# Attention with routed experts on one core: earlier routed chunks, sums over two steps, and an end in halves

## The chip, the core and the metric

The kernel runs on one core of a Trainium2 chip, as one launch. The metric is the device time of that launch in microseconds (us). Its engines are TensorE (PE, with weight loads as PEld), VectorE (DVE), ScalarE (ACT), GpSimd (POOL) and SyncE (SP, which here only issues DMAs). [...]

## The reference

The input x has 8 sequences of 512 tokens of 128 numbers. The output is x plus an attention layer plus a layer of experts, both fed with the same layer norm of x:

```python
xn = _layernorm(x)
# attention: 16 heads of 8 numbers, causal
w = softmax(q @ k.T / sqrt(8), masked below the diagonal)
attn = (w @ v) @ Wp + bp
# experts: the best 2 of 8 for each token, and one shared by all
ffn(x, g, u, d) = silu(x @ g.T) * (x @ u.T) @ d.T      # 352 hidden
routed = sum over the 2 chosen e of topw[e] * ffn(xn, expert e)
out = x + attn + ffn(xn, shared) + routed
```

## The kernel before

Tokens lie on the 128 partitions. A sequence has four tiles of 128 tokens (NC = 4), so there are 32 tiles (NT); `x_sb` holds them all in SBUF and collects the output: each part of the result is added into it.

**Steps.** The main loop runs over 32 sets n of four heads (a sequence b has four sets) and over five score tiles in each (`TILES`: two "wide", two "mixed", one "half"). That makes 160 steps, step = 5n + i. In a step, `weigh` lets TensorE fill a two-bank PSUM tile with scores (`fill`; the pool has a single buffer), and ScalarE takes one Exp over 1024 columns to `pT` (line 443). The diagonal blocks must be masked: in the first 40 steps TensorE adds a mask by small matmuls (L326), from step 40 (`BUSY`) GpSimd sets masked places to zero after Exp by an affine select (L451). In steps with i = 2, 4 and 0 of the next set, `attend` multiplies finished `pT` tiles by the values into the PSUM tile `av` (L466). The scores' row maxima, needed before a set's Exp, are made ahead by `look` for the step 11 later: TensorE matmuls into two banks (L365), two reduces on VectorE (L394, L400), and a cast on ScalarE that lays the mask down (L353). `shift` sends the maxima by three small DMAs into extra rows of q. The last maxima are taken in step 148.

**Attention's end.** After two sets, `evacuate` copies `av` to `o_sb` (ScalarE, L491); `divide` transposes it on TensorE (L500), takes reciprocals of the sums and multiplies (VectorE, L502, L506) into `a_new`. After a sequence's four sets, `turn` transposes `a_new` (L514) and copies it to `attT` (ScalarE, L515), and `join` multiplies by `wp_sb` (L537) and adds the product to `x_sb` (L541).

**Experts.** The work is a stream of 52 pairs of 128-row blocks: 13 shared pairs, 36 routed, 3 shared (`experts`). A pair has three chunks: TensorE gate and up matmuls (`gu`, one PSUM buffer, L611), a tanh on ScalarE (L616) and two VectorE operations (L617, L618). During the next pair's first two chunks it gets its two down projections (L638). A routed block's result is copied by ScalarE (L644) and scattered to a DRAM buffer `results` by GpSimd's indirect DMA (L622); a shared one is added to `x_sb` (L648). Where chunks run is set by a table: `chunks[step]` spreads k chunks evenly over a range of steps. The first chunk of a step stands after `look`, a second one at the step's end. Before: 39 shared chunks in steps -2 to 41, 108 routed in 42 to 145, 9 shared in 146 to 157.

**Collecting.** When all routed pairs are stored, each further step from the third on collects one sequence: two DMAs of 256 KB on SP's queue (`collect`, L706), which depend on all returns. `add_up` runs two steps (`LAG`) after, half a sequence a step, with a scalar_tensor_tensor on VectorE for each tile and choice (x += result * weight, L719). `due(step, f)` puts f into a step's side work, which `side` takes after that step's chunk and before up to two waiting down projections. `store` writes a sequence by SP (L726).

**After the last step** come the last attend and `evacuate`, the last pair's two down projections, what is still due (the last sums, `divide`, `turn`, `join`), and the stores of sequences 6 and 7.

The order on PE, DVE, ACT and SP is that of the program text. No planner moves it.

Of the kernel before, what the change touches and what calls it, by code (L numbers as in the profile page):

```python
# [11 lines left out]
F32 = mybir.dt.float32  # L12
# [3 lines left out]
ALU = mybir.AluOpType  # L16
# [9 lines left out]
P = 128  # L26
B, S, E = 8, 512, 128
H, D = 16, 8
NC = S // P
NT = B * NC  # L30
NG = H // 4
HH = H // 2
# [5 lines left out]
EARLY = 13  # L38
NE = 8
FF = 352  # L40
NF = 3
FP = NF * P
TOPK = 2
NP = TOPK * NT * P
BLK = P
MB = 2
# [4 lines left out]
BUSY = 40  # L51
# [3 lines left out]
LAG = 2  # L55
# [10 lines left out]
def attn_moe_kernel(  # L66
# [15 lines left out]
    nc = tc.nc  # L82
# [8 lines left out]
    x_sb = const.tile([P, NT, E], F32, name="x_sb")  # L91
# [8 lines left out]
    wp_sb = const.tile([E, E], F32, name="wp_sb")  # L100
# [22 lines left out]
    ident = const.tile([P, P], F32, name="ident")  # L123
# [4 lines left out]
    for i in range(NV):  # L128
        t = const.tile([P, NC, H, 32], F32, name=f"v_ext{i}")
# [6 lines left out]
    for i in range(NU):  # L136
        q = const.tile([P, HH, S], BF16, name=f"qs{i}")
        k = const.tile([P, HH, S], BF16, name=f"ks{i}")
# [19 lines left out]
    for m, sign in ((mask_q, 1), (mask_k, -1)):  # L158
        nc.gpsimd.memset(m, 0.0)
        nc.gpsimd.affine_select(  # L160
            out=m, in_=m, pattern=[[-sign, P]], compare_op=ALU.is_ge, fill=MASKED,
# [9 lines left out]
        out=before, in_=ones16, pattern=[[1, P]], compare_op=ALU.is_gt, fill=0.0,  # L171
# [6 lines left out]
    for e in range(NE):  # L178
# [5 lines left out]
        out=upto, in_=upto, pattern=[[1, NE], [-1, NE]], compare_op=ALU.is_ge, fill=0.0,  # L184
# [12 lines left out]
    attT = rows  # L197
    weight = const.tile([P, TOPK, NT], F32, name="weight")
# [8 lines left out]
    def pool(name, bufs, **kw):  # L207
        return ctx.enter_context(tc.tile_pool(name=name, bufs=bufs, **kw))
# [3 lines left out]
    at = pool("at", 2)  # L212
# [11 lines left out]
    def misc(shape, name, dtype=F32):  # L224
        return mi_ps.tile(shape, dtype, tag="mi", name=name)


    a_sb, in_dram, parts_of, first_dram = {}, {}, {}, []
# [64 lines left out]
    def fetch(u, h0=0, h1=HH):  # L293

        b, half = divmod(u, 2)
        heads = slice(half * HH + h0, half * HH + h1)
        rows_q, rows_k = in_dram[b]
        for r in range(3):
            nc.sync.dma_start(qs[u % NU][24 * r : 24 * r + 24, h0:h1], rows_q[:, heads])
        for r in range(3):  # L300
            d = nc.sync.dma_start(
                ks[u % NU][24 * r : 24 * r + 24, h0:h1], rows_k[8 * r : 8 * r + 24, heads]
            )
        return d.ins
# [134 lines left out]
    def weigh(n, kind, j, on_pool):  # L439

        ps = fill(n, kind, j, on_pool)
        pT = pr.tile([P, 2, S], F32, name="pT")
        last_exp[:] = [nc.scalar.activation(pT, ps, AF.Exp, scale=D**-0.5).ins]  # L443
        if on_pool:
            if kind == "half":
                diagonals = [pT.rearrange("p t (u k) -> p (t u) k", u=2)[:, :, :P]]
            else:
                diagonals = [pT[:, :, :P]] + ([pT[:, :, 3 * P :]] if kind == "mixed" else [])
            with tc.issue_after(sent[-1]):
                for d in diagonals:  # L450
                    nc.gpsimd.affine_select(  # L451
                        out=d, in_=d, pattern=[[0, d.shape[1]], [1, P]], compare_op=ALU.is_ge,
                        fill=0.0, base=0, channel_multiplier=-1,
                    )
        return pT
# [70 lines left out]
    def offset(b):  # L526
        xb = x_sb[:, ts(b, NC), :]
        with tc.issue_after(sent[-1]) if sent else ExitStack():
            nc.gpsimd.tensor_tensor(
                xb, xb, bias_sb.unsqueeze(1).to_broadcast([P, NC, E]), ALU.add  # L530
            )

    def join(b):

        ps = misc([P, NC, E], "p_ps")
        for c in range(NC):
            nc.tensor.matmul(  # L537
                ps[:, c], lhsT=attT[:, b * NC + c], rhs=wp_sb, start=True, stop=True
            )
        xb = x_sb[:, ts(b, NC), :]  # L540
        nc.vector.tensor_tensor(xb, ps, xb, ALU.add)  # L541


    stream = [("shared", j) for j in range(EARLY)]
# [155 lines left out]
    got = {}  # L700

    def collect(b):

        r = later_pools["got"].tile([P, TOPK, NC, E], F32, name="r")
        for i in range(TOPK):
            d = nc.sync.dma_start(  # L706
                r[:, i].rearrange("p c e -> p (c e)"),
                results[ds(i * NT * P + b * S, S)].rearrange("(p c) e -> p (c e)", p=P),
            )
            for x_ in returned:  # L710
                tc.add_manual_dep(d.ins, x_.name, SYNC, reason="any pair may be in any block")
        got[b] = r

    def add_up(b, c0, c1):

        for c in range(c0, c1):
            t = b * NC + c
            for i in range(TOPK):
                nc.vector.scalar_tensor_tensor(  # L719
                    x_sb[:, t, :], got[b][:, i, c], weight[:, i, t : t + 1], x_sb[:, t, :],  # L720
                    ALU.mult, ALU.add,
                )

    def store(b):

        nc.sync.dma_start(out[b].rearrange("(c p) e -> p c e", p=P), x_sb[:, ts(b, NC), :])  # L726
# [5 lines left out]
    total_steps = B * NG * NTILES  # L732
    ready = {}

    def due(step, f):
        ready.setdefault(step, []).append(f)
# [3 lines left out]
    def look(step, between=lambda: None):  # L740

        t = len(looked)
        if t >= total_steps:
            return lambda: None
        looked.append(step)
        n, i = divmod(t, NTILES)
        maxima(n, i, between)
        if i < NTILES - 1:
            return lambda: None
        if n == 0:  # L750
            return partial(shift_parts, n)
        if n < 4:
            return lambda: due(step + 1, partial(shift, n, shift_parts(n)))
        return lambda: first.setdefault(step + 2, []).append(partial(shift, n, shift_parts(n)))
# [16 lines left out]
    def begin(step):  # L771
        for f in first.pop(step, []):
            more = f()
            if more is not None:
                more()
# [310 lines left out]

    to_collect = list(range(B))

    first_step, routed_from, routed_to = -2, 42, 146
    chunks = {}  # L1090
    for a, z, k in (
        (first_step, routed_from, NF * EARLY),
        (routed_from, routed_to, NF * (NB // MB)),
        (routed_to, total_steps - 2, NF * (NT // MB - EARLY)),
    ):
        for m in range(z - a):
            chunks[a + m] = (m + 1) * k // (z - a) - m * k // (z - a)
# [6 lines left out]
    all_back = []  # L1104
# [6 lines left out]
    for t in range(FIRST):  # L1111
        step = t - FIRST
# [40 lines left out]
    for n in range(B * NG):  # L1153
        b, g = divmod(n, NG)
        waiting = []
        for i, (kind, j) in enumerate(TILES):
            step = n * NTILES + i
            begin(step)
            if step in fetches:
                fetch(fetches[step])  # L1160
            on_pool = step >= BUSY
            waiting.append((kind, j, weigh(n, kind, j, on_pool)))
            parts_then = look(step)
            some_chunks(step, False)
            if step in light:
                warm(5)
            parts_then()
            if step not in MORE and len(looked) < total_steps:
                prepare(*divmod(len(looked), NTILES))
            some_routing()  # L1170
            send_some()
            for f in late:
                f()
            late = []
            if i == 1 and n % 2 == 0:
                av = av_ps.tile([P, S], F32, name="av")
            if i in (1, 3, 4):
                late = [partial(attend, n, waiting, av)]
                waiting = []
            side(step, 2)  # L1180
            some_chunks(step, True)
            if step in MORE:
                look(step)()
                prepare(*divmod(len(looked), NTILES))
            if len(stored) == NB // MB:
                if not all_back:
                    for_routed.close()
                    later_pools["got"] = pool("got", 6)
                all_back.append(step)
            if to_collect and len(all_back) > 2:  # L1190
                at_b = to_collect.pop(0)
                collect(at_b)
                due(step + LAG, partial(add_up, at_b, 0, NC // 2))
                due(step + LAG + 1, partial(add_up, at_b, NC // 2, NC))

                if (at_b + 1) * NC <= MB * EARLY:
                    due(max(step + LAG + 2, last_shift), partial(store, at_b))
        if n % 2:
            late.append(partial(evacuate, n, av))
            due(step + 2, partial(divide, n))  # L1200
        if n % NG == 2 and b + 1 < B:
            due(step + 1, partial(offset, b + 1))
        if g == NG - 1:
            due(step + 3, partial(turn, b))
            due(step + 4, partial(join, b))
# [12 lines left out]
    for step in sorted(ready):  # L1218
        for f in ready[step]:
            more = f()  # L1220
            if more is not None:
                more()
    for b in to_collect:
        collect(b)
        add_up(b, 0, NC)
    for b in range(MB * EARLY // NC, B):
        store(b)


_OUT = (B, S, E)  # L1230
# [58 lines left out]
```

## Time and profile before

| | |
|---|---|
| runs | 620.67 us median of 3 (618.37 to 620.8) |
| profiled execution | 616.3 us, its span from first to last instruction 614.6 us |
| mean granted TensorE clock | 0.968 |
| busy: PE, DVE, ACT, POOL | 563.3, 463.3, 370.4, 244.0 us |
| Exp (L443), 160 of them | 164.1 us busy, 1026 ns each |
| sums of results (L719), 64 | 21.4 us busy |
| sums of products (L541), 8 | 5.4 us busy, 681 ns each |
| result loads (L706), 16 DMAs | 256 KB each |
| Exp of step 138 and of step 159 start | 533.6 and 596.6 us |

The profile gives one execution. A group's line has its source line, engine, operation and tiles, with count and durations in ns. In the digits over 40 slices each stands for 15.4 us, and 9 means 90% or more. In the timeline the first number is the start, the second the length, and the bracket tells how long the engine had been idle and what released it. Since each step has one Exp, in order, the rows of L443 date the steps.

### The profile page before, as it was taken

The numbers are of one execution on the slowest core, as the hardware profiler recorded it, in microseconds if no ns is written. First come the engines' busy times: TensorE is split into PE (matmuls) and PEld (weight loads), VectorE is DVE, ScalarE is ACT, GpSimd is POOL, SyncE is SP. The second block draws the span as 40 slices with busy tenths as digits, with TensorE's granted clock in tenths as the row PEclk, the third lists the DMA queues.
The fourth block names the chain that finished last, engine by engine and source line by source line (L and its number), as shares of the span: only waits on it lengthen the run. The fifth ranks groups of instructions, "written<-read, shape, count | busy, mean of one in ns | idle before, by whom it ended". The sixth has DMA issues, their size and how long they took to land.

```text
span 614.6 us, 13602 instructions
## 1 busy us (share of the span) xinstructions
PE 563.3 (92%) x4796; PEld 414.0 (67%) x4796; DVE 463.3 (75%) x1213; ACT 370.4 (60%) x668; POOL 244.0 (40%) x365
## 2 busy tenths in 40 slices
PE   6989598798999999999999999999999999999964
PEld 4656375566666677777776877777777877786533
DVE  7787867676768787777787778687788778876594
ACT  5735354463547666686667666586667766665530
POOL 9510444643557234333433344233434334433320
PEclk9989799998999999999999999999999999999986
DMA  7744244142143674838585785838585875720471
GB/s 219 229 117 172 95 109 109 37 131 78 37 121 110 197 225 135 233 106 251 178 240 159 223 233 166 217 93 250 178 218 194 238 232 145 215 96 3 138 223 51
DMA packets 52363, 98.38 MB, mean 160 GB/s; under 512 B 10054, under 2 KB 35530, under 8 KB 50136
## 3 DMA queue, kind: packets, MB, share of 16 engines
q1 hardware_dynamic: 46216, 83.78, 47.6%
q0 software_dynamic: 5360, 13.66, 6.4%
q8 instruction: 38, 0.62, 0.4%
q14 instruction: 29, 0.24, 0.1%
q10 hardware_dynamic: 720, 0.08, 0.1%
HBM read 73.36 MB, written 24.26 MB: 159 GB/s over the span
## 4 chain that ended last, share of the span: by engine, by line
PE 67%; ACT 6%; DVE 6%; issue 2%; POOL 0%; ACTq 0%; DVEq 0%
PE gu L611 19%; PE av L466 11%; PE y L638 11%; PE scT L322 9%; PE sc_diag L365 5%; PE sc_left L365 4%; DVE x_sb L719 3%; ACT pT L443 2%; PE qk_ps L239 2%; ACT sc_diag L353 2%; PE p_ps L537 1%; ACT th L616 1%; PE s_ps L585 1%; PE aT_ps L514 1%; PE mT_ps L423 1%
## 5 line engine op out<-in xcount | busy, mean ns | idle before, releaser
L443 ACT ACTIVATE pT<-scT 128x1024 f32<-128x1024 f32 x160 | 164.1, 1026 | 68.6 <-PE scT L322 27.3
L622 POOL DMA_INDIRECT results<-o,goes x72 | 73.1, 1015 | 129.7 <-ACT o L644 110.0
L451 POOL TENSOR_SCALAR_AFFINE_SELECT pT<-pT 128x256 f32<-128x256 f32 (+1 forms) x168 | 72.4, 447 | 118.7 <-ACT pT L443 115.6
L611 PE MATMUL gu<-sT,w 128*128 128x128 f32 x864 | 116.0, 277 | 2.3 <-PE sc_left L365 0.8
L394 DVE TENSOR_REDUCE peaks<-sc_diag 128x4 f32<-128x512 f32 x128 | 88.0, 688 | 38.1 <-PE sc_diag L365 25.7
L611 PEld LDWEIGHTS gu<-sT,w 128*128 128x128 f32 x864 | 108.0, 191 | 6.8 <-PE sc_diag L365 1.8
L322 PE MATMUL scT<-qs,ks 75*128 75x384 bf16 (+3 forms) x512 | 103.2, 303 | 3.9 <-ACT pT L443 3.8
L690 POOL DMA_INDIRECT slots<-rows_attT,slot x64 | 62.6, 979 | 81.2 <-issue 36.2
L616 ACT ACTIVATE th<-gu 128x256 f32<-128x256 f32 x156 | 59.8, 384 | 57.7 <-PE gu L611 39.7
L466 PE MATMUL av<-pT,v_ext 128*32 128x512 f32 (+3 forms) x1024 | 91.2, 452 | 1.0 <-POOL pT L451 1.0
L365 PEld LDWEIGHTS <-qs 72*128 72x128 bf16 x896 | 64.9, 98 | 38.8 <-issue 20.6
L617 DVE SCALAR_TENSOR_TENSOR th<-th,gu 128x256 f32<-128x256 f32 x156 | 65.1, 417 | 32.7 <-ACT th L616 30.5
L394 DVE TENSOR_REDUCE peaks<-sc_left 128x4 f32<-128x512 f32 x128 | 87.1, 680 | 0.0
L353 ACT CAST sc_diag<-mask_q 128x512 f32<-128x512 bf16 x117 | 69.2, 592 | 25.3 <-DVE peaks L394 17.9
L365 PE MATMUL sc_diag<-ks,qs 72*128 72x128 bf16 (+1 forms) x576 | 62.1, 225 | 12.4 <-ACT sc_diag L353 11.0
L618 DVE TENSOR_TENSOR h<-gu,th 128x256 f32<-128x256 f32 x156 | 66.2, 424 | 5.4
L638 PEld LDWEIGHTS y<-w,h 128*128 128x128 f32 x432 | 54.2, 191 | 23.4 <-issue 10.6
L638 PE MATMUL y<-w,h 128*128 128x128 f32 x432 | 64.4, 285 | 1.2 <-ACT v_ext L289 1.2
L365 PE MATMUL sc_left<-ks,qs 72*128 72x128 bf16 (+1 forms) x320 | 61.7, 274 | 3.2 <-DVE peaks L394 3.1
L322 PEld LDWEIGHTS <-ks 75*128 75x128 bf16 x512 | 46.8, 99 | 23.7 <-issue 12.5
L611 PE MATMUL gu<-xnT,ws_sb 128*128 128x256 f32 x192 | 54.1, 406 | 3.3 <-DVE h L618 3.2
L466 PEld LDWEIGHTS av<-pT,v_ext 128*32 128x32 f32 x1024 | 23.6, 109 | 32.2 <-issue 21.6
(166 smaller groups left out, 634.5 us busy)
## 6 DMA issues: line engine op xcount, KB each, us to landing
w<-in_w_exp_dram SPq DMA_DIRECT2D x72, 576.0 KB
qs<-dq SPq DMA_DIRECT2D x45, 192.0 KB
ks<-dk SPq DMA_DIRECT2D x45, 192.0 KB
slots<-empty POOLq DMA_DIRECT2D x6, 780.0 KB
s<-slots SPq DMA_DIRECT2D x33, 130.0 KB
r<-results SPq DMA_DIRECT2D x16, 256.0 KB
dq<-parts SPq DMA_DIRECT2D x7, 384.0 KB
dk<-parts SPq DMA_DIRECT2D x7, 384.0 KB
```

Of the source, the lines that this page charges most:

```text
L322: nc.tensor.matmul(out_, lhsT=k[: QK + 3, ts(i, P)], rhs=q[: QK + 3, i * P :], start=True, stop=bare)
L353: nc.scalar.copy(diag_ps.rearrange("p (b k) -> p b k", k=P), mask_q.unsqueeze(1).to_broadcast([P, NC, P]),)
L365: nc.tensor.matmul(out_, lhsT=q[:QK, ts(c, P)], rhs=k[:QK, keys], start=start, stop=stop, skip_group_check=True,)
L394: nc.vector.tensor_reduce(peaks[:, i, 8 + 4 * t : 12 + 4 * t], banks[t].rearrange("p (b k) -> p b k", k=P), AX.X, ALU.max,)
L443: last_exp[:] = [nc.scalar.activation(pT, ps, AF.Exp, scale=D**-0.5).ins]
L451: nc.gpsimd.affine_select(out=d, in_=d, pattern=[[0, d.shape[1]], [1, P]], compare_op=ALU.is_ge, fill=0.0, base=0, channel_multiplier=-1,)
L466: nc.tensor.matmul(av[32 * jj : 32 * jj + 32, c * P :], lhsT=v_ext[b % NV][:, c, 4 * g + jj, :], rhs=weights, start=(n % 2 == 0 and c == 0 ...
L611: nc.tensor.matmul(gu[:, i, part], lhsT=w[c][:, ds(i * FP + f * P, P)], rhs=sT[:, part], start=True, stop=True,)
L616: nc.scalar.activation(th, gu[:, 0], AF.Tanh, scale=0.5)
L618: nc.vector.tensor_tensor(h[:, f], gu[:, 1], th, ALU.mult)
L622: d = nc.gpsimd.indirect_dma_start(results, bass.IndirectOffsetOnAxis(ap=goes_of[k][:, c : c + 1], axis=0), o, None, bounds_check=NP - 1, ...
L638: nc.tensor.matmul(y, lhsT=h[:, f, ts(c, P)], rhs=w[c % len(w)][:, ds(2 * FP + f * P, P)], start=(f == 0), stop=(f == NF - 1),)
```

## The change

Four edits:

1. The routed chunks are spread over steps 42 to 137 (96 steps rather than 104), and the nine last shared ones over 138 to 155 (18 rather than 12).
2. A sequence is collected every other step. Its second choices are weighed in place by ScalarE (four multiplications by a per-token weight), its first choices are still weighed and added by VectorE, tile by tile, in the same step; one step later a single 128x512 addition on VectorE takes in the second choices. The store of sequence 6 is now due in step 159; those of 0 to 5 stay due four steps after their collection, and not before step 153.
3. In steps 157 to 159 the scores are masked by TensorE, as in the first forty steps.
4. The last two sets' `evacuate`, `divide`, `turn`, `join` and the last store are replaced by `finish`, which runs them as two halves of 256 tokens, with copies divided between ScalarE and VectorE, and stores one half from SP and the other from ScalarE's queue. It stands behind all other work.

```diff
+    def project_out(b, c0, k):
+        ps = misc([P, k, E], "p_ps")
+        for c in range(k):
+            nc.tensor.matmul(
+                ps[:, c], lhsT=attT[:, b * NC + c0 + c], rhs=wp_sb, start=True, stop=True
+            )
+        return ps
...
+    def finish(n, av):
+
+        b, g = divmod(n, NG)
+        o_sb = at.tile([P, S], F32, name="o_sb")
+        half = S // 2
+        k = NC // 2
+        a_new = a_sb[b]
+        copies = (nc.scalar.copy, nc.vector.tensor_copy)
+        ots, aTs, outs = [], [], []
+        for i in range(2):
+            copies[i](o_sb[:, ts(i, half)], av[:, ts(i, half)])
+        for i in range(2):
+            ot = misc([P, k, HH, 16], "ot")
+            for c in range(k):
+                nc.tensor.transpose(
+                    ot[:, c].rearrange("p k s -> p (k s)"), o_sb[:, ts(k * i + c, P)], ident
+                )
+            ots.append(ot)
+        for i, ot in enumerate(ots):
+            rden = at.tile([P, k, HH, 1], F32, name="rden")
+            nc.vector.reciprocal(rden, ot[:, :, :, D : D + 1])
+            nc.vector.tensor_tensor(
+                a_new[:, ts(i, k), ts(g // 2, HH * D)].rearrange("p c (k d) -> p c k d", d=D),
+                ot[:, :, :, :D], rden.to_broadcast([P, k, HH, D]), ALU.mult,
+            )
+        for i in range(2):
+            ps = misc([E, half], "aT_ps")
+            for c in range(k):
+                nc.tensor.transpose(ps[:, ts(c, P)], a_new[:, k * i + c, :], ident)
+            aTs.append(ps)
+        for i, ps in enumerate(aTs):
+            copies[i](
+                attT[:, ds(b * NC + k * i, k)], ps.rearrange("e (c p) -> e c p", c=k)
+            )
+        for i in range(2):
+            outs.append(project_out(b, k * i, k))
+        for i, ps in enumerate(outs):
+            these = ds(b * NC + k * i, k)
+            nc.vector.tensor_tensor(x_sb[:, these, :], ps, x_sb[:, these, :], ALU.add)
+            (nc.sync, nc.scalar)[i].dma_start(
+                out[b].rearrange("(c p) e -> p c e", p=P)[:, ts(i, k)], x_sb[:, these, :]
+            )
...
-    def add_up(b, c0, c1):
-
-        for c in range(c0, c1):
+    def weigh_second(b):
+
+        for c in range(NC):
+            nc.scalar.mul(got[b][:, 1, c], got[b][:, 1, c], weight[:, 1, b * NC + c : b * NC + c + 1])
+
+    def add_up(b, i):
+
+        if i:
+            xb = x_sb[:, ts(b, NC), :]
+            nc.vector.tensor_tensor(xb, xb, got[b][:, 1], ALU.add)
+            return
+        for c in range(NC):
             t = b * NC + c
-            for i in range(TOPK):
-                nc.vector.scalar_tensor_tensor(
-                    x_sb[:, t, :], got[b][:, i, c], weight[:, i, t : t + 1], x_sb[:, t, :],
-                    ALU.mult, ALU.add,
-                )
+            nc.vector.scalar_tensor_tensor(
+                x_sb[:, t, :], got[b][:, 0, c], weight[:, 0, t : t + 1], x_sb[:, t, :],
+                ALU.mult, ALU.add,
+            )
...
-    first_step, routed_from, routed_to = -2, 42, 146
+    first_step, routed_from, routed_to = -2, 42, 138
...
-        (routed_to, total_steps - 2, NF * (NT // MB - EARLY)),
+        (routed_to, total_steps - 4, NF * (NT // MB - EARLY)),
...
-            on_pool = step >= BUSY
+            on_pool = BUSY <= step < total_steps - 3
...
-            if to_collect and len(all_back) > 2:
+            if to_collect and len(all_back) > 2 and len(all_back) % 2:
                 at_b = to_collect.pop(0)
                 collect(at_b)
-                due(step + LAG, partial(add_up, at_b, 0, NC // 2))
-                due(step + LAG + 1, partial(add_up, at_b, NC // 2, NC))
+                due(step + LAG, partial(weigh_second, at_b))
+                due(step + LAG, partial(add_up, at_b, 0))
+                due(step + LAG + 1, partial(add_up, at_b, 1))
 
                 if (at_b + 1) * NC <= MB * EARLY:
                     due(max(step + LAG + 2, last_shift), partial(store, at_b))
+                elif at_b < B - 1:
+                    due(total_steps - 1, partial(store, at_b))
+        if n == B * NG - 1:
+            continue
...
-    for b in to_collect:
-        collect(b)
-        add_up(b, 0, NC)
-    for b in range(MB * EARLY // NC, B):
-        store(b)
+    assert not to_collect
+    finish(B * NG - 1, av)
```

`join` calls `project_out` for its matmuls and is otherwise as before.

More of the change, by code (lines that the diff above doesn't have):

```diff
@@ L531, in offset @@
             )
-    def join(b):
[L535 to L538, printed above, removed]
-            )
+    def project_out(b, c0, k):
[5 more added lines that the diff above has]
+        return ps
+    def join(b):
+        ps = project_out(b, 0, NC)
@@ L712, in collect @@
         got[b] = r
-    def add_up(b, c0, c1):
-        for c in range(c0, c1):
-            t = b * NC + c
-            for i in range(TOPK):
-                nc.vector.scalar_tensor_tensor(
-                    x_sb[:, t, :], got[b][:, i, c], weight[:, i, t : t + 1], x_sb[:, t, :],
-                    ALU.mult, ALU.add,
-                )
+    def weigh_second(b):
[7 more added lines that the diff above has]
+        for c in range(NC):
+            t = b * NC + c
+            nc.vector.scalar_tensor_tensor(
+                x_sb[:, t, :], got[b][:, 0, c], weight[:, 0, t : t + 1], x_sb[:, t, :],
+                ALU.mult, ALU.add,
+            )
     def store(b):
```

## The prediction

> **What bounds the kernel now.** I read the page first, for the stretch where TensorE stops being the bound. Columns are 40 slices of the span.
>
> ```profile
> span 614.6 us, 13602 instructions
> PE 563.3 (92%) x4796; PEld 414.0 (67%) x4796; DVE 463.3 (75%) x1213; ACT 370.4 (60%) x668; POOL 244.0 (40%) x365
> PE   6989598798999999999999999999999999999964
> DVE  7787867676768787777787778687788778876594
> PEclk9989799998999999999999999999999999999986
> ```
>
> TensorE is full until the last few slices; there VectorE is full instead. Busy time by stretch (us, then PE, PEld, DVE, ACT, POOL with counts, clock, DMA share, GB/s) places the change of bound:
>
> ```profile
> 500.00:550.00 50.00, 49.70 (x460) 37.77 (x459) 38.78 (x99) 33.44 (x63) 20.10 (x35) 1.00 0.57 179
> 580.00:590.00 10.00, 6.97 (x49) 4.14 (x48) 8.66 (x26) 4.34 (x6) 2.34 (x5) 0.92 0.67 221
> 590.00:600.00 10.00, 7.86 (x58) 4.40 (x57) 9.54 (x29) 4.16 (x6) 2.37 (x5) 0.84 0.64 192
> 600.00:614.60 14.60, 6.07 (x28) 4.97 (x26) 6.94 (x22) 0.75 (x2) 0.00 (x0) 0.62 0.18 54
> ```
>
> The rows of the summing line, and the chain of waits from 560 us on, name the work:
>
> ```profile
> L719 DVE SCALAR_TENSOR_TENSOR x_sb<-r,weight,x_sb x64: 339/351/722, 578.6 to 605.5; 128x128 f32<-128x128 f32 x64
> by line: DVE x_sb L719 32.4%; PE gu L611 9.1%; issue 7.4%; PE av L466 5.3%; DVE h L618 4.6%; PE scT L322 4.4%; PE y L638 4.3%; DVE th L617 4.1%; PE p_ps L537 3.7%; ACT th L616 2.1%; PE aT_ps L514 2.0%; ACT pT L443 1.9%; DVE x_sb L648 1.4%;
> ```
>
> All 64 sums run in the last 36 us (21.4 us busy, 0.335 each back to back). The timeline shows what they hold up: Exp, one a step and so a clock of the steps, and then the end.
>
> ```profile
> 585.98 1.02 ACT L443 ACTIVATE pT<-scT 128x1024 f32<-128x1024 f32 x1 [1.52 <-PE scT L322]
> 590.58 0.38 ACT L616 ACTIVATE th<-gu 128x256 f32<-128x256 f32 x1 [3.58 <-PE gu L611]
> 592.32 1.02 ACT L443 ACTIVATE pT<-scT 128x1024 f32<-128x1024 f32 x1 [1.35 <-PE scT L322]
> ...
> 596.60 1.02 ACT L443 ACTIVATE pT<-scT 128x1024 f32<-128x1024 f32 x1 [0.74 <-PE scT L322]
> ```
>
> Counted back from the last one (step 159 at 596.60), steps 138, 146, 149 and 155 start their Exp at 533.6, 560.7, 569.1 and 583.2. So from step 138 to 159 are 63.0 us, and 18.0 more to the end of the span, of which the output row waits for the sums until 605.8.
>
> [...]
>
> **The change, part by part.** Unit costs are start to start in the timeline of a full TensorE:
>
> ```profile
> 552.17 0.39 PE L365 MATMUL sc_diag<-ks,qs 72*128 72x128 bf16 x4
> 552.39 0.38 PE L365 MATMUL sc_left<-ks,qs 72*128 72x128 bf16 x2
> 552.61 1.06 PE L611 MATMUL gu<-sT,w 128*128 128x128 f32 x8
> 553.60 1.07 PE L466 MATMUL av<-pT,v_ext 128*32 128x384 f32 x16
> ```
>
> Scores for maxima 0.44, a routed chunk 0.99, attend 1.00 (0.57 for the half tile). From the same view: fill 0.44, a down projection 0.86, a shared chunk 0.88, turning a_new or the sums 0.44, projecting out 0.88, a mask matmul 0.06.
>
> *Steps 42 to 137.* Before, 99 routed chunks are done by step 137, now 108. Added: 9 x 0.99, 6 downs x 0.86, one turn of slots 0.22, together 14.3; TensorE is 97% busy here, so they cost their length, and I add 0.6 for waits on the one gu buffer in steps with two chunks. Measured beside it: the 20 steps from 42 on have no second chunk and take 67.1 us; the next three twenties have one each and take 68.8, 70.1 and 67.8, so 1.7, 3.0 and 0.7 a chunk. Bounds: 6.3 to 27. I take 14.9: step 138 starts at 548.5. VectorE goes from 2.6 of 3.38 us a step to 2.7 of 3.53, ScalarE and the weights' DMA (share 0.57 to 0.74) by 4 to 8%: none becomes the bound.
>
> *Steps 138 to 148.* Shared chunks are in odd steps only, 139 to 155. A step without a chunk can't be as short as its matmuls: the single score buffer makes fill wait for Exp, and the next Exp for fill. Steps 150 and 153 show that floor, 1.75; with maxima and the cast between, step 146 took 1.94. A step after such a one took 0.36 over its sum (step 147: 3.62 worked out, 3.98 measured). So 138 to 144: 1.9, 3.9, 1.95, 3.3, 2.5, 2.85, 2.1 = 18.5. Before, TensorE was dense in these steps; this thinning is the cost of the first part.
>
> The results are stored in step 141, so sequences are collected in 143, 145 to 157, and summed two steps later. In 145 and 147 VectorE has reduces 1.29, chunk 0.85, four sums 1.34, a down's sum 0.28: 3.76; ScalarE Exp, tanh, cast and four weighings. [...] bounds 1.08 (as L644's copies, 0.27) and 1.66 (as L854, 0.41 net). They stand ahead of the next Exp. Steps 145 to 148: 3.7, 2.1, 3.9, 1.9 = 11.6. The single 128x512 sum of even steps (0.68) lies under the floor.
>
> *Steps 149 to 158.* No maxima. An odd step is now ScalarE's: fill and gu 1.42, tanh after Exp, 1.27 of weighing, then Exp: 2.8; an even one 1.75. Masks by TensorE: 4 x 0.06 on each of three fills (0.24), and GpSimd's select no longer follows Exp (0.4 to 0.8 a tile; hidden except in the last step). Sum 4 x 2.8 + 3 x 1.75 + 2.0 + 2.4 + 2.0 = 22.9. Step 159 starts at 601.5, 4.9 later than before.
>
> *The end.* From that Exp: 1.02, attend to 1.65, twelve down matmuls to 3.4. VectorE then has the second down's sum (3.8), the last 128x512 sum (4.5) and, behind it in its queue, the copy of half of the output sums (4.9); the reciprocals and products of halves (0.25 and 0.29 each, from 0.35 and 0.42 whole) end at 6.0; turn, copy, product, add of the second half at 6.4, 6.85, 7.45, 7.9. The store and the closing waits took 3.3 after L541: 11.2 in place of 18.0. End 601.45 + 11.2 = 612.7, against 614.6. The sums' 64 instructions become 32 and eight.
>
> *Queues.* SP runs ahead of the steps. The first collect waits for the last returned rows and stands ahead of the three small writes of row maxima for group 30 (issued in step 145, wanted in 150): five steps of slack cover it. Four stores in 153 (0.39 each) stand ahead of a collect; it issues in 0.95, lands 2.2 after, about 3.5 into step 153, and is wanted 6 into it. If that cover fails, the weighing waits, and Exp behind it: 1 to 2 us, once. GpSimd only loses work.
>
> **Rivals.** *Cheap chunks* (faster): the added chunks fill TensorE's 2.4% of idle and cost 1.2 each, midway between 0.7 and 1.7: 10.8 for 14.9, span 608.6, time 614.6. For it: window 102 to 122. Against: TensorE left only 0.08 us idle a step. *Dear chunks* (slower): where two chunks share a step, the second waits for VectorE to free gu; at 2.4 each, between the mean of the three windows (1.8) and the dearest (3.0), 21.6 for 14.9: span 619.4, time 625.4. It decides from 1.9 a chunk on (no gain), and over 0.5% slower from 2.2. Against: in step 145 the second gu group began without a wait. *The backlog stays*: if collects land late, VectorE's 64 x 0.335 shrink only to 32 x 0.335 + 8 x 0.68 = 16.2 and the gain at the end is 5 us, not 11: about 619 in span; I count it with the dear case.
>
> **How the numbers follow.** The profiled execution took 616.3 (span 614.6); the median of the runs is 620.67. I scale by the spans: 620.67 x 612.7 / 614.6 = 618.7. Half a per cent, what a measurement here can tell, is 3.1. The likeliest case has 0.5 and its own range 615.8 to 621.5 (2 us on the weighings and floors, 1.5 on the chunks): 0.14 of it faster, 0.35 same, 0.01 slower. Cheap chunks 0.3: 0.28 faster, 0.02 same. Dear or late 0.2: 0.14 slower, 0.06 same. Together 0.42, 0.43, 0.15; range 612.5 to 624.5.
>
> **What would show it.** Exp of step 138 at 548 to 549 and of step 159 at 600 to 603; L719's successor with 32 small and eight large rows, begun by 570, VectorE never over 85% after; ScalarE's weighings near 0.3 net, odd steps from 149 on about 1 us longer than even ones; 11 us from the last Exp to the end. Wrong if step 138 is off by over 3 us, or if a weighing waits for a collect.

## The result, and the profile after

The changed kernel takes 629.31 us (median of 4 runs, 627.07 to 630.28), the kernel before 619.52 beside it: ratio 1.0154, 95% interval 1.0113 to 1.0195. It is slower by about 10 us. The profiled execution has a span of 625.4 us, before 614.6. The forecast was 618.7, range 612.5 to 624.5: the measured time lies above that range, and slower was the direction to which the prediction gave only 0.15. The profiled execution is the fastest of the four (627.07).

The page of the changed kernel answers to the lines shown of before.

```profile
span 625.4 us, 13626 instructions
PE 566.8 (91%) x4808; PEld 413.0 (66%) x4808; DVE 457.2 (73%) x1194; ACT 379.8 (61%) x700; POOL 241.8 (39%) x360
PE   7879698798989999999899999999899999998885
DVE  6787776776768887777577767776676767777974
PEclk8999799998999999999799999999999999999999
```

In this execution TensorE's clock no longer falls at the end. VectorE still has one slice of 9 there (578 to 594 us), as before. In the middle TensorE has slices of 8 where before were nines, and one with a clock of 0.7. Busy time over steps 42 to 137 (columns as before), first before, then after:

```profile
209.20:533.60 324.40, 316.90 (x2880) 243.26 (x2878) 251.59 (x631) 222.07 (x414) 124.18 (x200) 1.00 0.69 199
```

```profile
209.70:563.00 353.30, 336.36 (x2992) 258.62 (x2990) 257.89 (x651) 228.47 (x430) 129.23 (x206) 0.99 0.66 188
```

This stretch grew by 28.9 us where 14.9 was forecast. TensorE's idle time in it went from 7.5 us (324.4 - 316.9) to 16.9. What follows it is shorter, as forecast:

| us | before | forecast | after |
|---|---|---|---|
| Exp of step 42 to Exp of step 138 | 324.4 | 339.3 | 353.3 |
| Exp of step 138 to Exp of step 159 | 63.0 | 53.0 | 51.4 |
| Exp of step 159 to the end of the span | 18.0 | 11.2 | 10.9 |

The parts that were meant for the end give back 18.7 us; the denser routed stretch takes 28.9.

Take each step's time after minus the same step's before. The growth stands at the steps with two chunks (49, 57, 65 and so on, every eighth, here called double steps) and the step behind each: +1.1 and +1.1 at 49 and 50, +2.0 and +0.7 at 73 and 74, +1.0 and +2.2 at 121 and 122. Two are worse: +1.7 and +4.9 at 65 and 66, +1.7 and +2.8 at 105 and 106. Elsewhere steps differ by 0.6 us at most, up or down, except where before had a double step of its own or the step behind it (68, 93, 94, 119 and 120, now 0.7 to 1.9 shorter) and at 135 (0.8 shorter). Part of the growth is the added work; two causes lie behind the rest.

**The gu buffer.** The timeline of the changed kernel, steps 49 and 50; the gu group at 235.16 is the second chunk, that at 237.73 the next step's.

```profile
235.16 1.13 PE L658 MATMUL gu<-sT,w 128*128 128x128 f32 x8
236.33 0.38 ACT L663 ACTIVATE th<-gu 128x256 f32<-128x256 f32 x1 [0.84 <-PE gu L658]
236.74 0.42 DVE L664 SCALAR_TENSOR_TENSOR th<-th,gu 128x256 f32<-128x256 f32 x1 [1.73 <-ACT th L663]
237.03 1.02 ACT L443 ACTIVATE pT<-scT 128x1024 f32<-128x1024 f32 x1 [0.32 <-PE scT L322]
237.06 0.38 PE L365 MATMUL sc_left<-ks,qs 72*128 72x128 bf16 x2
237.20 0.42 DVE L665 TENSOR_TENSOR h<-gu,th 128x256 f32<-128x256 f32 x1
237.73 1.13 PE L658 MATMUL gu<-sT,w 128*128 128x128 f32 x8 [0.29 <-PE sc_left L365]
```

From the end of the second chunk's matmuls its tanh and VectorE's two operations take until 237.62, and only then may the one gu buffer be written again: the next chunk starts at 237.73. Between them TensorE has a small transpose, fill and maxima scores alone. The line names the last thing on its own engine as what ended the wait; the time of h (L665) shows the true one.

**Late weights.** The same kernel's timeline in step 66, and SP's queue before it. Each gu group of eight takes four matmuls from either block's weights.

```profile
297.07 0.46 PE L658 MATMUL gu<-sT,w 128*128 128x128 f32 x2 [0.56 <-PE sc_left L365]
299.19 1.65 PE L658 MATMUL gu<-sT,w 128*128 128x128 f32 x6 [1.67 <-DMA w<-in_w_exp_dram]
301.06 1.49 PE L685 MATMUL y<-w,h 128*128 128x128 f32 x6
```

```profile
283.28 0.36 SPq L606 DMA_DIRECT2D w<-in_w_exp_dram  x1
283.74 1.15 SPq L299 DMA_DIRECT2D qs<-dq  x3
284.94 1.49 SPq L301 DMA_DIRECT2D ks<-dk  x3
287.54 0.38 SPq L606 DMA_DIRECT2D w<-in_w_exp_dram  x1
```

The second block's weights are issued at 287.54, behind six fetches of q and k (192 KB each), and the chain of waits has them landing 11.61 us later. The chunk waits 1.67, and what comes after is slow: six gu matmuls take 1.65, six y matmuls 1.49 in place of 0.94. In the record the clock is at 0.50 from 298.5 to 305.4, so it falls while the chunk waits (297.5 to 299.2); below are the stretch before and the first half of that one (columns as before).

```profile
295.11:298.53 3.42, 1.86 (x15) 1.16 (x13) 2.04 (x4) 1.41 (x2) 1.36 (x2) 1.00 0.89 267
298.53:301.94 3.41, 2.75 (x13) 2.75 (x14) 0.61 (x2) 1.07 (x3) 0.00 (x0) 0.50 0.87 318
```

With three pairs in eight steps and a fetch every ten, the two meet in this phase (by the code) only at the fetches of steps 64 and 104, just the places with the larger loss.

The end is as forecast. The weighing, from the rows of its line:

```profile
L764 ACT ACTIVATE r<-r,weight x32: 385/391/403, 584.7 to 616.2; 128x128 f32<-128x128 f32 x32
```

### The profile page after: what moved, and what is told of

Read it like the earlier page. It is cut to its first block, busy times and chain, and to the rows that moved or that the text cites. A ratio compares the mean times of both kernels' runs of the same rounds, so it can differ in the third digit from the quotient of the medians.

```text
span 625.4 us, 13626 instructions
## 1 busy us (share of the span) xinstructions
PE 566.8 (91%) x4808; PEld 413.0 (66%) x4808; DVE 457.2 (73%) x1194; ACT 379.8 (61%) x700; POOL 241.8 (39%) x360
## 4 chain that ended last, share of the span: by engine, by line
PE 65%; ACT 7%; DMA 4%; DVE 3%; issue 2%; SPq 0%; POOL 0%; ACTq 0%; DVEq 0%
PE gu L658 20%; PE y L685 10%; PE av L466 10%; PE scT L322 9%; PE sc_diag L365 5%; PE sc_left L365 4%; DMA w<-in_w_exp_dram 4%; ACT pT L443 2%; PE qk_ps L239 2%; ACT sc_diag L353 2%; PE s_ps L632 1%; ACT th L663 1%; PE p_ps L536 1%; ACT rest L246 1%; PE scT L326 1%
## 5 line engine op out<-in xcount | busy, mean ns | idle before, releaser
L658 PE MATMUL gu<-sT,w 128*128 128x128 f32 x864 | 119.0, 280 | 10.2 <-DMA w<-in_w_exp_dram 3.2
L451 POOL TENSOR_SCALAR_AFFINE_SELECT pT<-pT 128x256 f32<-128x256 f32 (+1 forms) x163 | 70.4, 447 | 115.9 <-ACT pT L443 112.9
L665 DVE TENSOR_TENSOR h<-gu,th 128x256 f32<-128x256 f32 x156 | 66.2, 424 | 5.3
L322 PEld LDWEIGHTS <-ks 75*128 75x128 bf16 x512 | 46.5, 98 | 25.7 <-issue 14.3
L658 PE MATMUL gu<-xnT,ws_sb 128*128 128x256 f32 x192 | 52.5, 397 | 0.4 <-DVE h L665 0.3
```

The source lines that it names most:

```text
L322: nc.tensor.matmul(out_, lhsT=k[: QK + 3, ts(i, P)], rhs=q[: QK + 3, i * P :], start=True, stop=bare)
L451: nc.gpsimd.affine_select(out=d, in_=d, pattern=[[0, d.shape[1]], [1, P]], compare_op=ALU.is_ge, fill=0.0, base=0, channel_multiplier=-1,)
L658: nc.tensor.matmul(gu[:, i, part], lhsT=w[c][:, ds(i * FP + f * P, P)], rhs=sT[:, part], start=True, stop=True,)
L665: nc.vector.tensor_tensor(h[:, f], gu[:, 1], th, ALU.mult)
```

## The experiments

Theories. A: the denser stretch costs more than its work, because a second chunk in a step makes the next wait for the gu buffer. B: it does so because weights come late behind a fetch. C (rival to both): the stretch isn't the trouble; ScalarE's weighing, or the end, is. The experiments ran on three chips, with medians of the kernel before of 620.2 (first four), 609.7 (next four) and 608.7 (last three), so ratios are compared, and stretches inside the profiles. The chips differ ahead of these stretches: Exp of step 42 starts at 208 to 212 us in the profiles of the first four and at 198 to 202 in the others. Each experiment has one profiled execution, so what a profile shows of a single wait needn't hold in every execution. "The stretch" is Exp of step 42 to Exp of step 138.

### The routed chunks late again

```diff
-    first_step, routed_from, routed_to = -2, 42, 138
+    first_step, routed_from, routed_to = -2, 42, 146
-        (routed_to, total_steps - 4, NF * (NT // MB - EARLY)),
+        (routed_to, total_steps - 2, NF * (NT // MB - EARLY)),
-            if to_collect and len(all_back) > 2 and len(all_back) % 2:
+            if to_collect and len(all_back) > 2:
```

> The changed kernel with its first part undone: routed chunks in steps 42 to 145 again, shared ones in 146 to 157, one sequence collected every step from 150 on; weighing by ScalarE, masks by TensorE and the end in halves stay. If the denser routed stretch is what costs (steps 42 to 137 took 353 us, before 324), Exp of step 138 comes back to 534 and the end is a little shorter than before, since VectorE has 16.2 us of sums in place of 21.4: span 607 to 611, ratio to before 0.985 to 0.995. If the loss is instead in ScalarE's weighing or in the end, it stays at or above before: ratio 1.00 to 1.01.

610.93 us, ratio 0.9826 (0.9745 to 0.9906). Steps 42 to 137 take 330.0 us, 138 to 159 61.0, the end 10.9. C falls: without the first part the rest of the change is a gain of 1.7%. The stretch is 5.5 over before, 3.3 of it in step 68, where a chunk waited 1.6 us for weights; in steps 57 and 89 chunks waited 0.7 each. So in this execution, the slowest of the four, B struck the less dense schedule too.

### The first part alone

The kernel before with `routed_to` 138 and the shared chunks up to 155.

> The kernel before with the first part alone: routed chunks in steps 42 to 137, shared ones in 138 to 155, everything else as before (a sequence collected every step, eight sums each on VectorE). If the denser stretch costs 29 us by itself, step 138 starts at 562 to 564 as in the changed kernel, and the ratio is 1.015 to 1.03. If the cost needs the other parts, step 138 starts below 552 and the ratio is at most 1.00.

639.41 us, ratio 1.0329 (1.0241 to 1.0418), a little more than was expected. The stretch takes 349.7 us, so it costs by itself, with no weighing in sight. The sums of two choices on VectorE then fall, one sequence a step, among steps that still have chunks; VectorE is full all the same, and TensorE's clock falls in the middle of it:

```profile
595.00:605.00 10.00, 6.84 (x34) 3.22 (x27) 9.48 (x32) 3.02 (x4) 1.46 (x3) 0.67 0.00 1
```

From step 138 to 159 are 62.0 us, hardly less than before: VectorE's sums had to become fewer, not only earlier. The end is 11.9 with the old end, its sums being done by then.

### Weights a chunk sooner

```diff
-            for name, bufs in (("wexp", 3 * MB), ("inp", 3), ("goes", 4)):
+            for name, bufs in (("wexp", 3 * MB + 1), ("inp", 3), ("goes", 4)):
             yield partial(chunk, k, 0), [partial(down, k - 1, 0)] if k else []
+            load_weights(k + 2, 0)
...
-            load_weights(k + 2, 0)
+            load_weights(k + 2, 1)
...
-            load_weights(k + 2, 1)
```

> The changed kernel with the experts' weights asked for one chunk sooner, in seven buffers rather than six. Theory of late weights (two chunks of steps 66 and 106 waited for a load that stood behind the fetch of q and k in SP's queue, and the clock fell after the first): 5 to 7 us off, step 138 at 556 to 558, ratio to before 1.003 to 1.008. Theory of the gu buffer (every step with two chunks makes the next one wait for VectorE): at most 3 us off, ratio 1.010 to 1.015.

621.40 us, ratio 1.0021 (0.9998 to 1.0044). The stretch takes 346.3 us, 7.0 less; the steps 66 and 106 cost +1.0 each in place of +4.9 and +2.8, step 67 is 1.0 shorter, and no chunk waits for a load. The clock stays at 1.00 in the stretch, so the 7.0 hold the slow matmuls too. B holds, for half of the 14.0 us (28.9 less 14.9) that were missing from the forecast. The double steps cost what they did (+2.0 and +0.7 at 73 and 74), and TensorE still idles 13.7 us.

### The second chunk sooner in its step

```diff
-            side(step, 2)
-            some_chunks(step, True)
+            some_chunks(step, True)
+            side(step, 2)
```

> The changed kernel with the second chunk of a step placed before the step's side work (down projections, sums), so that these stand on TensorE between it and the next step's chunk. Theory of the gu buffer: the waits of 0.56 to 0.81 us after each of the twelve double steps go, 6 to 10 us off, step 138 at 553 to 557, ratio 1.000 to 1.006. Theory of late weights: no more than 1 us off, step 138 at 562 or later, ratio 1.014 to 1.017.

629.58 us, ratio 1.0127 (1.0049 to 1.0205), the stretch 352.9: no gain in the stretch, against what theory A was taken to say here. The ratio by itself would suit theory B; the timeline shows why it doesn't speak against A; the step's first chunk is at 350.82 and the second at 353.46.

```profile
350.82 1.06 PE L658 MATMUL gu<-sT,w 128*128 128x128 f32 x8
352.89 0.42 DVE L665 TENSOR_TENSOR h<-gu,th 128x256 f32<-128x256 f32 x1
353.46 1.13 PE L658 MATMUL gu<-sT,w 128*128 128x128 f32 x8 [1.58 <-DVE h L665]
```

The wait has moved ahead of the second chunk: with one buffer it is paid on one side or the other. The expectation was wrong, since it looked at one side only. This profile also has a wait for weights of 2.9 us in step 106.

### A buffer of its own for the second chunk

With the sooner weights, the second chunk of a step takes its PSUM tile from the pool of the small products:

```diff
-        gu = gu_ps.tile([P, 2, PAIR], F32, tag="gu", name="gu")
+        if second:
+            gu = misc([P, 2, PAIR], "gu2")
+        else:
+            gu = gu_ps.tile([P, 2, PAIR], F32, tag="gu", name="gu")
```

> The changed kernel with weights asked for a chunk sooner, and the second chunk of a step in a PSUM buffer of its own (from the pool of the small products) rather than the one gu buffer. Theory of the gu buffer: what is left of the excess in steps 42 to 137 (346 us with sooner weights, 338 to 340 by work alone) is the next chunk's wait for VectorE after a double step; it goes, TensorE's idle time there falls from 13.7 to 7 or 8 us, the stretch to 339 to 341, ratio to before 0.988 to 0.996. Rival (a second chunk simply is dearer than its 1.6 us of work, or ScalarE's order delays the next Exp): the stretch stays at 345 to 347, ratio 1.000 to 1.004.

604.16 us, ratio 0.9899 (0.9843 to 0.9956), not overlapping the 1.0021 (0.9998 to 1.0044) without it. The stretch of this kernel:

```profile
201.10:538.70 337.60, 329.40 (x2992) 255.51 (x2990) 256.67 (x651) 228.91 (x431) 129.80 (x206) 1.00 0.67 198
```

337.6 us, 8.7 less than with the sooner weights alone; TensorE's idle time is 8.2 us, near the 7.5 of before. The chunk behind a double step follows at once; steps 49 and 50 again:

```profile
226.44 1.06 PE L663 MATMUL gu<-sT,w 128*128 128x128 f32 x8
227.42 0.24 PE L423 MATMUL mT_ps<-ident,m_parts 128*48 128x128 bf16 x1
227.59 0.60 PE L322 MATMUL scT<-qs,ks 75*128 75x512 bf16 x2
...
228.48 1.06 PE L663 MATMUL gu<-sT,w 128*128 128x128 f32 x8
```

2.04 us from one group to the next, where it was 2.57. A holds. Of the 8.7 us, 5.5 are idle time of TensorE and 3.2 time in which it counts as busy, at the same clock of 1.00; no run shows why busy time shrinks.

The second buffer also takes away the waits that the kernel before had at its own three double steps, so the work of nine chunks is not simply what is left of 28.9. The less dense schedule with the same two remedies ("Late again, with sooner weights and the second buffer", below) gives it:

```profile
201.53:523.48 321.95, 316.43 (x2882) 243.36 (x2880) 251.13 (x632) 221.99 (x414) 123.70 (x200) 1.00 0.69 202
```

Nine chunks cost 337.6 - 322.0 = 15.6 us there, forecast as 14.3. The same remedies take 324.4 - 322.0 = 2.4 off the stretch of before. So 28.9 = 7.0 (late weights) + 6.3 (waits on gu, 8.7 less 2.4) + 15.6 (work).

### Late again, with sooner weights

> Routed chunks in 42 to 145 and a collection every step as in the first experiment, with weights asked for a chunk sooner. If the waits for weights also cost the less dense schedule now and then (its profile showed one of 1.6 us in step 68 with 3.3 us lost), ratio 0.975 to 0.982; if they cost only the dense one, 0.982 to 0.985 as without.

599.84 us, ratio 0.9840 (0.9780 to 0.9899), against 0.9826 without the sooner weights. The stretch takes 324.7 us, what it took before, and no chunk waits for a load; but the medians show no gain from it. That is the second of the two expectations, with intervals too wide to exclude a small gain.

### Ending in step 141

Routed chunks in 42 to 141, a collection every step, sooner weights.

> As the kernel before in this call, with the routed chunks ending in step 141 rather than 145. Five more chunks before step 138 at 2.4 us each make that stretch 336 us; the sums begin four steps earlier. Theory that an end earlier only thins TensorE's last steps: same or slower than ending in 145 by up to 0.5%, ratio 0.978 to 0.988. Theory that VectorE's sums still hold up the last steps there: faster by 2 to 4 us, ratio 0.970 to 0.977.

604.41 us, ratio 0.9912 (0.9882 to 0.9943), slower than ending in 145 by 0.7%, a little more than either theory had. The intervals of the ratios just overlap, but on the same chip all eight runs (603.17 to 606.56) are slower than all four of the experiment above (596.77 to 601.28). The stretch is 336.1 us (expected 336), the steps to 159 56.3, the end 10.2. Eleven more microseconds before step 138 return five after it.

### The kernel before with sooner weights

> The kernel before with weights asked for a chunk sooner, nothing else. Its profile shows no chunk waiting for weights, so by the theory that late weights are a matter of the denser schedule alone: ratio 0.998 to 1.002. If a fetch ahead of a load delays it in some executions of the kernel before as well: 0.993 to 0.998.

608.11 us, ratio 0.9967 (0.9945 to 0.9990): a small gain, just clear of noise. That a load is late now and then in the kernel before too would account for it, but isn't shown: in the profile of the kernel before no chunk waits for one, in this kernel's one waits 0.7 us even so, and the stretch takes 326.1 us here, 324.4 before.

### Late again, with sooner weights and the second buffer

> Routed chunks in 42 to 145, a collection every step, weights asked for a chunk sooner, and the second chunk of a step in a PSUM buffer of its own. Only four steps have a second chunk there, three of them before step 138; at 0.7 to 0.9 us each the buffer is worth 2 to 3 us on top of the 0.984 measured without it: ratio 0.976 to 0.983. If a second chunk's wait doesn't matter in the less dense schedule: 0.983 to 0.986.

597.02 us, ratio 0.9805 (0.9767 to 0.9843): the lowest ratio of all, faster than both kernels. The stretch takes 322.0 us. Against 0.9840 (0.9780 to 0.9899) without the buffer the difference is as expected in size (2.7 us in the stretch), though the intervals overlap.

### The sums as before

The first experiment's kernel, with `add_up` of the kernel before, so that VectorE weighs and adds both choices.

> The first experiment's kernel with the sums as before: VectorE weighs and adds both choices, eight instructions a sequence, half a sequence a step; ScalarE weighs nothing. If the gain of the first experiment (0.983) comes from the shorter backlog on VectorE, 5 us are lost: ratio 0.989 to 0.994. If it comes from the end in halves and the masks alone: 0.982 to 0.986.

607.60 us, ratio 0.9978 (0.9955 to 1.0001). Nearly all of the gain is gone, more than the 5 us expected: Exp of step 157 follows that of 156 after 7.2 us again (2.8 in the first experiment), steps 138 to 159 take 65.0 in place of 61.0 and the end 14.5 in place of 10.9. The eight matmuls of the last product take 1.75 us on its chain of waits, 1.39 in the first experiment's timeline, so slow matmuls are part of it. Without the weighing by ScalarE the end in halves and the masks show no gain clear of noise. Whether the weighing gains as much with the old end was not run.

### The masks by GpSimd

The first experiment's kernel with `on_pool = step >= BUSY`.

> The first experiment's kernel with the last three tiles masked by GpSimd again. The select after the last Exp took 0.7 to 0.8 us on the path before, and three fills are 0.24 us shorter: about even, ratio 0.982 to 0.985. If the masks by TensorE were what shortens the end: 0.987 or more.

603.42 us, ratio 0.9919 (0.9896 to 0.9943), against 0.9826 (0.9745 to 0.9906) with the masks on TensorE: dearer than expected, though the intervals overlap a little. From the last Exp to the end it takes 13.7 us in place of 10.9 (10.9 also in the fastest kernel, on the same chip as this one). The last window, first with GpSimd's masks and then (first experiment) with TensorE's:

```profile
590.00:600.80 10.80, 5.87 (x32) 4.85 (x28) 5.02 (x16) 0.75 (x2) 0.00 (x0) 0.66 0.17 49
```

```profile
602.00:613.00 11.00, 5.87 (x52) 3.68 (x44) 6.56 (x20) 2.86 (x8) 0.00 (x0) 1.00 0.27 78
```

The select itself takes 0.69 us on the path. The rest goes with the clock: with GpSimd's masks TensorE waits 1.23 us before the last attend, its mean clock is 0.66 in the last window, and the twelve down matmuls take 2.52 us rather than 1.60. Whether the clock falls at this place in every execution isn't shown.

## Why the prediction was wrong

**Steps 42 to 137: the step that failed.** The prediction put the nine added chunks at "their length", 14.3 us, and 0.6 for waits on the gu buffer, because TensorE is 97% busy. The length was about right (15.6). The waits on gu added 6.3 us, not 0.6, and late weights another 7.0, where the text had the weights' DMA as no bound and so put it at nothing. Three readings led there.

- It had the measurement that told: the windows with a double step, 1.7, 3.0 and 0.7 us a chunk. In the trace before, each of the three holds a wait on gu: 0.56 us in step 68, behind the double step 67; 0.81 before the second chunk of step 93 and 0.55 in step 94; 0.29 in step 120. That is 2.2 us in all. The changed kernel's trace has waits of the same sizes at its double steps, 6.9 us in all. The 0.6 of the prediction is about the size of one of them.
- The argument against dear chunks ("in step 145 the second gu group began without a wait") looked at the wrong group. The second follows the first by attends and downs, and waits (0.81 us) only in steps 73 and 113. The third, in the next step, follows the second by 0.88 us of matmuls, while tanh and two VectorE operations take 1.2 by their durations. In step 146, behind the only double step that it looked at, there was no chunk. The count of those steps (twelve, not three) times that wait was there to be worked out: nine more at 0.74, the mean of the three before, are 6.6 us.
- The DMA share (0.69 of the stretch) says nothing of one load behind one fetch. The queue's order and the two periods, eight steps and ten, were in the code. What was missed is that they meet.

**Dear chunks, the slower rival.** Its size, 2.4 us a chunk or 21.6, is what the stretch grew by once weights were on time (346.3 - 324.4 = 21.9). That is in part luck, since 2.4 was taken midway between two readings of three windows. Its mechanism, a wait for VectorE to free gu, is the one shown, though mostly it is not the second chunk that waits but the next step's. Late weights came on top, 3.2 a chunk in all (28.9 / 9). It stood with a chance of 0.2 together with another case. **The backlog stays** didn't happen in the changed kernel: no weighing waited for its load. **Cheap chunks** fell.

**Steps 138 to 148 and 149 to 158.** Forecast 30.1 and 22.9, measured 30.3 and 21.1. The floor of 1.75 to 1.95 for steps without a chunk held, and so did the author's estimate of 1.27 for the four weighings of a step (between the bounds of 1.08 and 1.66): 1.27 was measured, 0.391 for one. Odd steps from 149 to 155 took 2.4 to 2.6 us, not 2.8. The 32 small and eight large sums came as said, but from 585.1 us on, not by 570, since step 138 was 14.5 us later than forecast. VectorE was busy 95% of the ten us from 584 on, where the prediction had it never over 85%.

**The end.** 11.2 forecast, 10.9 measured, for the reason given: VectorE's last 128x512 sum (0.69 us) stands ahead of its half of the copy. TensorE's clock stays at 1.00 there in this execution, which the sum neither named nor priced. In the kernel before its mean is 0.62 from 600 us on, with no gap of TensorE over 2.25 us.

**Masks.** Put at even but for the last step; worth 2.8 us at the end in the profiles, 0.7 of it the select, the rest with the clock. **Queues.** SP's part around the collects held: in the changed kernel's profile no weighing waited for a load on the path. In the profile with sooner weights one did, for 0.57 us, the case that was priced at 1 to 2 us once.

**The direction of the trade.** The forecast saw that thinning TensorE's last steps costs as much as it brings. With both waits mended the dense schedule is still slower than the late one (0.9899 against 0.9805). Ending in 141 is slower than ending in 145 too (0.9912 against 0.9840, both without the second buffer; with it, ending in 141 was not run). No run here shows a reason to end the routed chunks sooner once VectorE's sums are lighter.

## What to carry to other kernels

When work is added to an engine that is nearly full, cost its buffers and its loads as well as its length: look for the shortest distance between two users of a single buffer in the new order, not at the mean, and for where two periods in one DMA queue meet. A wait that a reordering removes on one side of an instruction can reappear on the other; only a second buffer removed it here. And test the parts alone: three of these four parts gain 1.7%, and the fourth turned that into a loss.

## What the runs showed of the hardware

TensorE's recorded clock has two values in the traces of the two kernels, 1.00 and 0.50; a figure such as 0.66 is a mean. It stays at half for 3.41 or 6.83 us at a time, and for 11.23 at the end of the kernel before. In the changed kernel it fell at 298.53 us, during the second of two waits of 0.56 and 1.67 us (step 66). In the run with GpSimd's masks its mean is 0.66 from 590 us on, where the timeline from 586.5 us on shows no wait of TensorE longer than 1.28 us. A wait of 1.74 us in the changed kernel, up to 609.48, went by at 1.00.

In the two traces a fall came after a stretch in which TensorE had little to do. From 85 us on there are six falls. In the 3.41 us before each, TensorE was busy 35% (fall at 148.00 us), 28% (588.32), 49% (598.56) and 27% (605.39) of the time in the kernel before, 41% (148.34) and 54% (298.53) in the changed one. After 56% (448.71 to 452.12) and 59% (605.73 to 609.15) in the changed kernel the clock stayed at 1.00. What decides is not shown, nor why the same place is slow in one execution and not in another.

A weight load of 576 KB landed 11.6 us after its issue when six fetches of 192 KB stood ahead of it in the same queue. In the changed kernel's DMA records the fetches' 8 KB packets start from 287.3 to 296.5 us. Of the 248 packets of a weight load's size (4608 bytes) that start between this load's issue and its landing, 155 come behind them. The DMA engines were 92% busy in these 11.6 us and moved 228 GB/s, other transfers included.
